# Softmax denominators by one weight sum per block, with three additions done by accumulating DMA transfers

## The chip, the cores and the metric

The kernel runs on one core of one Trainium2 chip. The metric is the device time of one execution in microseconds. The core's engines are TensorE (PE in the profile; PEld is its weight load), VectorE (DVE), ScalarE (ACT), GpSimd (POOL) and SyncE (SP), which only issues DMA transfers here. Each engine takes its instructions in the order of the program and waits on semaphores for the others.

## The reference, cut to what matters

Four layers follow one another on x of shape (16, 384, 16, 16), all in float32. The change is in the first, an attention over tokens, with 2 batches of 2048 tokens, 12 heads of 32 channels:

```python
xt = x.reshape(B, NUM_FRAMES, C, H, W).transpose(0, 2, 1, 3, 4)
xt = xt.reshape(B, C, N).transpose(0, 2, 1)
qk = (xt @ qk_w.T).reshape(B, N, 2, nh, HEAD_DIM)
...
attn = jax.nn.softmax(jnp.einsum('bhnd,bhmd->bhnm', q * scale, k), axis=-1)
attn = alpha * eye + beta * attn - gamma * Cm
out = jnp.einsum('bhnm,bhmd->bhnd', attn, v)
```

v is xt itself, and Cm is a matrix of 1/N, so the kernel computes alpha * x + beta * (exp(scores) v) / (sum of exp(scores)) - gamma * mean(x). The second layer (l1) is a depthwise 7x7 convolution, a LayerNorm and an MLP of 384 to 1536 to 384 with a response normalization; the third (l2) fuses gradients of the image through a 1x1 convolution; the fourth (l3a, l3b, l3c) holds 1x1 and 3x3 convolutions, a linear attention and a second MLP.

## The kernel before, in words

Channels lie on partitions, 3 groups of 128; tokens are the free dimension, in 4 blocks of 512 per batch. The kernel has two stages.

**Attention** (`attention`, from L398). A unit is a batch and a group of 4 heads; there are 6 units with 4 query blocks each, so 24 blocks. A block has 16 steps, one for each 128 keys. `scores` (L463) makes 4 matmuls, one per head, into two PSUM tiles of two banks (`pst`, three such tiles), and two exponentials on ACT, each over 1024 elements per partition. `weighted` (L481), run one step later so that ACT has time, multiplies by the values into `av`. In float32 each matmul is two MATMUL records in the profile, so a step has 8 records named st and 8 named av. For the softmax's denominator, DVE adds the exponentials of ADDS[n] successive steps, and `weights` (L524) lets PE multiply that sum by a matrix of ones into `dn`; ADDS gives 16, 8, 4 or 2 steps for each block, and a sum that is not the block's last one is multiplied in four quarters of 128 columns, spread over later steps. The sums use a pool of their own (`sp`, 4 tiles), the exponentials eight tiles of half a step (`ep`).

`finish` (L536) copies `dn` to SBUF on ACT, inverts it on DVE in four parts of 128 columns, scales the accumulated values and adds alpha * x. The dictionary `due` keeps work that is to be issued at a later step. `project` (L569) makes the queries and keys of blocks to come, two at a time, at step SLOT = 5 of a block, 12 MATMUL records; values come by DMA on SP's queue.

DVE would idle in part of this stage. So `fill` (L1481) puts work of the second layer there, after each step: one convolution task, and two `leads`, the l1 tasks of the first two images, whose LayerNorm starts at step LEAD. `pace` (L194) tells `fill` what a step costs PE and DVE by its own table, and what is left is filled.

**The rest.** Tasks of all 8 images are put into one order by a planner: each operation has an engine, a length and buffers that it takes and gives, and among the operations that can start soonest (within SLACK) the task of lowest RANK goes first. TURNS groups images that use the same MLP weights; `wa` and `wb` hold three chunks of 768 KB each, loaded by SP when their buffers come free. Within an engine the order of issue is then fixed; `InOrder` pins it, and its line (L96) is the line of nearly all records.

At the start, `first_loads` (L646) loads the first group's weights and then x, block by block, on SP's queue, and the vectors of scales and biases on ACT's.

```python
for n in range(NBLK):
    for t in range(NQC):
        es = scores(n, t)
        added = 0.0
        if before:
            before()
        before = lambda f=weighted, a=(n, t, es): f(*a)
        if t == SLOT and steps:
            added = project(f"p_{u}_{n}", steps[:2])
            del steps[:2]
        fill((u * NBLK + n) * NQC + t, added)
```

Of the kernel before, what the change touches and what calls it, by code (L numbers as in the profile page):

```python
# [9 lines left out]
F32 = mybir.dt.float32  # L10
# [3 lines left out]
PSUM = bass.MemoryType.PSUM  # L14

P = 128
# [15 lines left out]
SLOT = 5  # L32
LEAD = 20 * NQC + 6
# [12 lines left out]
RANK = {  # L46
    "mid": ((36.6, 22.0, 24.3, 85.6), (18.6, 42.9, 96.6, 26.9)),
    "l1": ((50.1, 89.5, 75.2, 4.0), (51.1, 16.8, 81.7, 28.5)),
    "l3c": ((45.7, 99.2, 100.9, 121.0), (-20.9, -6.3, 70.9, 62.0)),
    "conv": 109.4,  # L50
}
SLACK = 0.196
JUNK = 2

ADDS = (16, 8, 16, 16, 4, 4, 4, 2, 2, 8, 16, 16, 4, 16, 2, 4, 16, 8, 4, 4, 4, 4, 4, 4)
# [61 lines left out]
class Plan:  # L117
# [24 lines left out]
    def run(self, op):  # L142
# [9 lines left out]
        for tag, n in op.gives:  # L152
            self.room[tag] = sorted(self.room[tag] + [op.ready] * n)
# [40 lines left out]
def pace(t):  # L194


    n, i = divmod(t - 1, NQC)
    adds = ADDS[n]
    pe, dve = 2.066, 2.275 if t and i % adds else 0.0
    at = i - adds - 1  # L200
    parts = sum(j * adds // 4 == at % adds for j in range(4)) if at >= 0 else 0
    if parts:
        pe += 0.22 * parts
    elif i == 1 and n > 0:
        pe += 0.87
    else:
        pe += 0.09
    if n > 0:
        dve += {2: 0.88, 3: 0.88, 4: 0.88, 5: 0.88, 6: 0.6, 7: 0.66}.get(i, 0.0)
    return pe, dve  # L210
# [187 lines left out]
def attention(tc, X, xt, L0, block, small, col, cols, ones, load_qk, banks, fill, bound):  # L398
# [6 lines left out]
    with ExitStack() as actx:  # L405
# [48 lines left out]
        due = {}  # L454

        def unit(u, made, gm):
# [3 lines left out]
            adds = ADDS[u * NBLK : (u + 1) * NBLK]  # L460
            acc, sums = {}, {}

            def scores(n, t):  # L463
                es = []
                for i in range(2):
                    es.append(ep.tile([P, 2, BLK], F32, tag="e", name=f"e_{u}_{n}_{t}_{i}"))
# [10 lines left out]
                for i in range(2):  # L477
                    act.activation(es[i], sts[i], AF.Exp, scale=HD**-0.5)
# [1173 lines left out]
```

## Time and profile before

| | us |
|---|---|
| median of 3 runs | 2679.8 (2679.11 to 2679.9) |
| the profiled execution's own time | 2679.38 |
| its span | 2677.6 |
| PE busy | 2644.6 (99%) |
| DVE busy | 2011.5 (75%) |
| ACT busy | 1557.5 (58%) |
| POOL busy | 7.4 (0%) |
| exponentials e<-st, 768 of 128x1024 | 743.2 |
| additions s<-s,e and s<-e,e, 606 of 128x1024 | 513.3 + 191.0 |
| denominator matmuls dn<-s,ones | 2016 records |

The profile is one execution. Its groups name an operation as out<-in with its shape, the number of instructions, the busy time, the mean of one in ns, and then the idle time ahead of them with what ended it. Busy PE time is not all work: records of pipelined matmuls overlap, so the time of a step is read from the starts in the timeline.

### The profile page before, as it was taken

How to read it: one execution, taken by the hardware profiler on the slowest of the kernel's cores; microseconds unless marked ns; L12 is line 12 of the kernel's file. 1: busy time of each engine (PE TensorE's matmuls, PEld its weight loads, DVE VectorE, ACT ScalarE, POOL GpSimd, SP SyncE). 2: the span in 40 equal slices, each digit the busy share in tenths (PEclk: the TensorE clock that was granted, in tenths of full speed). 3: DMA queues.
4: the chain of work that ended last, by engine and by line, in shares of the span. 5: the costliest groups of instructions: out<-in, count | busy, mean ns of one | idle time of the engine just before them, and what ended most of it. 6: DMA issues, size and time to landing. Idle time of an engine off the chain costs nothing. (4 is left out here: it accounts for less than half of the span.)

```text
span 2677.6 us, 32803 instructions
## 1 busy us (share of the span) xinstructions
PE 2644.6 (99%) x12997; PEld 1061.5 (40%) x12997; DVE 2011.5 (75%) x2588; ACT 1557.5 (58%) x2314; POOL 7.4 (0%) x54
## 2 busy tenths in 40 slices
PE   8999999999999999899999999999999999999999
PEld 2223333233323323345444454444444444454443
DVE  5999999999999889999999999999652202732300
ACT  6787878878787888564565335457443542625201
POOL 0000000000000000000000000000000000000000
PEclk9999999999999999999999999999999999999999
DMA  3000000000000003000001001011001110000000
GB/s 150 5 13 1 9 9 5 13 1 5 13 1 1 1 13 108 23 0 0 1 1 47 25 12 31 29 36 36 24 24 36 47 36 24 0 1 1 12 17 20
DMA packets 28851, 55.69 MB, mean 21 GB/s; under 512 B 1680, under 2 KB 14096, under 8 KB 28688
## 3 DMA queue, kind: packets, MB, share of 16 engines
q1 hardware_dynamic: 28544, 53.35, 6.0%
q8 instruction: 104, 1.70, 0.3%
q14 instruction: 59, 0.48, 0.1%
q10 hardware_dynamic: 144, 0.15, 0.0%
HBM read 47.21 MB, written 6.29 MB: 20 GB/s over the span
## 5 line engine op out<-in xcount | busy, mean ns | idle before, releaser
L96 ACT ACTIVATE e<-st 128x1024 f32<-128x1024 f32 x768 | 743.2, 1025 | 88.5 <-PE st L96 80.7
L96 DVE SCALAR_TENSOR_TENSOR y<-l,vec,y 128x420 f32<-128x420 f32 (+8 forms) x1152 | 660.0, 638 | 5.0
L96 DVE TENSOR_TENSOR s<-s,e 128x1024 f32<-128x1024 f32 x444 | 513.3, 1216 | 11.7 <-ACT e L96 11.2
L96 PE MATMUL st<-q,k 32*128 32x512 f32 x3072 | 474.1, 641 | 4.0 <-ACT e L96 2.3
L96 PE MATMUL av<-e,v 128*32 128x512 f32 x3072 | 410.9, 606 | 4.3 <-ACT va L96 4.2
L96 PE MATMUL ph_l<-y,wa 128*128 128x512 f32 x576 | 261.4, 597 | 0.0
L96 PE MATMUL ph_l3c<-d_l3c,wa 128*128 128x512 f32 x576 | 258.4, 593 | 0.0
L96 PE MATMUL po_l<-hid_l,wb 128*128 128x512 f32 x576 | 255.7, 596 | 1.1 <-ACT hid_l L96 1.1
L96 PE MATMUL po_l3c<-hid_l3c,wb 128*128 128x512 f32 x576 | 256.6, 593 | 0.0
L96 PEld LDWEIGHTS st<-q,k 32*128 32x128 f32 x3072 | 146.1, 183 | 220.1 <-issue 132.4
L96 DVE TENSOR_TENSOR s<-e,e 128x1024 f32<-128x1024 f32 x162 | 191.0, 1221 | 54.7 <-ACT e L96 36.0
L96 ACT ACTIVATE hid_l<-ph_l,vec 128x512 f32<-128x512 f32 x96 | 66.0, 687 | 202.9 <-PE ph_l L96 202.8
L96 ACT ACTIVATE hid_l3c<-ph_l3c,vec 128x512 f32<-128x512 f32 x96 | 65.6, 687 | 202.6 <-PE ph_l3c L96 202.5
L96 PEld LDWEIGHTS av<-e,v 128*32 128x32 f32 x3072 | 60.6, 108 | 298.1 <-issue 274.0
L96 DVE SCALAR_TENSOR_TENSOR o_l3c<-po_l3c,vec,l 128x512 f32<-128x512 f32 x24 | 17.5, 748 | 209.6 <-PE po_l3c L96 208.8
L96 PEld LDWEIGHTS po_l<-hid_l,wb 128*128 128x128 f32 x576 | 109.5, 191 | 139.1 <-issue 128.0
L96 PEld LDWEIGHTS ph_l3c<-d_l3c,wa 128*128 128x128 f32 x576 | 108.8, 190 | 137.2 <-issue 133.4
L96 PEld LDWEIGHTS ph_l<-y,wa 128*128 128x128 f32 x576 | 109.1, 191 | 136.0 <-issue 125.1
L96 PEld LDWEIGHTS po_l3c<-hid_l3c,wb 128*128 128x128 f32 x576 | 109.0, 190 | 134.6 <-issue 132.8
L96 PE MATMUL p<-x,wqk_sb 128*128 128x512 f32 x288 | 132.3, 610 | 1.2 <-DMA x<-in_x_dram 1.2
L96 DVE SCALAR_TENSOR_TENSOR g_l3a<-h_l3a,dw,g_l3a 128x450 f32<-128x450 f32 (+1 forms) x192 | 119.0, 702 | 4.2 <-ACT g_l3a L96 4.1
L96 PEld LDWEIGHTS dn<-s,ones 128*32 128x32 f32 x2016 | 64.1, 110 | 125.4 <-issue 107.0
(155 smaller groups left out, 2446.3 us busy)
## 6 DMA issues: line engine op xcount, KB each, us to landing
wa<-in_w_dram SPq DMA_DIRECT2D x9, 768.0 KB, 4.5
wb<-in_w_dram SPq DMA_DIRECT2D x9, 768.0 KB, 5.0
wa<-in_mlp_w_dram SPq DMA_DIRECT2D x9, 768.0 KB, 4.4
wb<-in_mlp_w_dram SPq DMA_DIRECT2D x9, 768.0 KB, 4.5
x<-in_x_dram SPq DMA_DIRECT2D x8, 768.0 KB, 10.6
v<-in_xt_dram SPq DMA_DIRECT2D x24, 256.0 KB, 2.7
out_dram<-o_l3c SPq DMA_DIRECT2D x24, 256.0 KB, 2.1
qkv<-in_qkv_wT_dram SPq DMA_DIRECT2D x3, 576.0 KB, 11.1
```

Source lines behind the costliest of these rows:

```text
L96: self.last = self.tc.keep_in_program_order(make(*args, **kw))
```

## The change

- **One weight sum per block.** All 16 steps of a block are added up before PE multiplies once by ones. An exponential tile now holds a whole step (four heads, 2048 elements per partition), and there are six of them. The sum is built in place in step 2's tile.
- **Three additions by transfers.** The tiles of steps 1, 6 and 10 are added to those of steps 0, 5 and 9 by an accumulating DMA on GpSimd's queue; DVE merges the results into the sum at steps 6 and 10 and after the block's end (MERGED).
- **Banks.** PSUM is one pool of eight single banks, for scores, av, dn, projections and the second layer's statistics. Each head has an exponential of its own, of 512 elements.
- **Reciprocals.** The sums of a block, equal over the 32 rows of a head, go to DRAM and come back as a tile of 16 columns; that is inverted, written out and read back spread over the rows. The last block is divided in full instead.
- **Projections** move from step 5 to step 0 of a block; up to block PAIRED (21) the last merge, the denominator and `finish` of the block before follow them there; later blocks have these at steps 0 to 3 of the next block. The leads' ScalarE work (`fill` called with None) is issued ahead of them, and the first lead starts at step 17 * 16 + 1.
- **Start.** Keys' weights and x by channel group are loaded first; the vectors come on SP's queue; the batch-norm constants are computed after the loads are issued.
- **The rest of the kernel** has other TURNS (8 groups instead of 6), other RANK, SLACK and AFTER. A weight chunk of `wb` is given back by the user that comes last in the order, counted by `spent`.

The diff, cut to its core:

```diff
-SLOT = 5
-LEAD = 20 * NQC + 6
+PAIRED = (NB * NC - 1) * NBLK + 1
+LEAD = (17 * NQC + 1, 20 * NQC + 6)
 FIRST = NQC + 10
 TURNS = (
     (0, ((0, 0), (0, 1), (0, 2), (0, 3),)),
-    (1, ((0, 0), (0, 1),)),
-    (0, ((1, 0), (1, 2),)),
-    (1, ((0, 2),)),
-    (0, ((1, 1), (1, 3),)),
-    (1, ((1, 0), (0, 3), (1, 2), (1, 1), (1, 3),)),
+    (1, ((0, 0),)),
+    (0, ((1, 0),)),
+    (1, ((0, 1),)),
+    (0, ((1, 2), (1, 3),)),
+    (1, ((1, 0),)),
+    (0, ((1, 1),)),
+    (1, ((0, 2), (1, 2), (1, 1), (0, 3), (1, 3),)),
 )
-AFTER = ('x4', 0, 2)
+AFTER = ('x4', 0, 1)
...
-ADDS = (16, 8, 16, 16, 4, 4, 4, 2, 2, 8, 16, 16, 4, 16, 2, 4, 16, 8, 4, 4, 4, 4, 4, 4)
+MERGED = {0: 6, 5: 10, 9: NQC}
...
-        ep = pool("ep", 8)
-        sp = pool("sp", 4)
+        ep = pool("ep", 6)
         op = pool("op", 2)
-        pst = pool("pst", 3, space=PSUM)
-        pacc = pool("pacc", 1, space=PSUM)
-        def bank2(name):
-            return pst.tile([P, 2, BLK], F32, tag="st", name=name)
-        banks.append(lambda name: bank2(name)[:, 0, :])
-        fill(-1)
+        pb = pool("pb", 8, space=PSUM, reuse_waits="tile")
+        dp = pool("dp", 2, space=DRAM)
+        def bank(name):
+            return pb.tile([P, BLK], F32, tag="bank", name=name)
+        banks.append(bank)
...
+        due, behind, late = {}, [], []
         def unit(u, made, gm):
...
-            adds = ADDS[u * NBLK : (u + 1) * NBLK]
-            acc, sums = {}, {}
+            acc = {}
             def scores(n, t):
-                es = []
-                for i in range(2):
-                    es.append(ep.tile([P, 2, BLK], F32, tag="e", name=f"e_{u}_{n}_{t}_{i}"))
-                sts = [bank2(f"st_{u}_{n}_{t}_{i}") for i in range(2)]
+                es = ep.tile([P, 4, BLK], F32, tag="e", name=f"e_{u}_{n}_{t}")
+                sts = [bank(f"st_{u}_{n}_{t}_{h}") for h in range(4)]
                 for h in range(4):
...
-                for i in range(2):
-                    act.activation(es[i], sts[i], AF.Exp, scale=HD**-0.5)
+                for h in range(4):
+                    act.activation(es[:, h, :], sts[h], AF.Exp, scale=HD**-0.5)
                 return es
             def weighted(n, t, es):
                 if t == 0:
-                    acc["av"] = pacc.tile([P, BLK], F32, tag="av", name=f"av_{u}_{n}")
+                    acc["av"] = bank(f"av_{u}_{n}")
                 for h in range(4):
...
-                at = t % adds[n]
-                for i in range(2):
-                    if at == 0:
-                        sums[i] = es[i]
-                    elif at == 1:
-                        s = sp.tile([P, 2, BLK], F32, tag="s", name=f"s_{u}_{n}_{t}_{i}")
-                        dve.tensor_tensor(s, sums[i], es[i], ALU.add)
-                        sums[i] = s
+                block = u * NBLK + n
+                k = block * NQC + t
+                end = t == NQC - 1
+                pairs = [p for p in MERGED if MERGED[p] < NQC or block < NB * NC * NBLK - 1]
+                if t in pairs:
+                    acc[t] = es
+                elif t - 1 in pairs:
+                    nc.gpsimd.dma_start(acc[t - 1], es, accum_op=ALU.add)
+                    def merge(other=acc[t - 1], sums=acc):
+                        dve.tensor_tensor(sums[2], sums[2], other, ALU.add)
+                    when = MERGED[t - 1]
+                    if when == NQC and block < PAIRED:
+                        late.append(merge)
                     else:
-                        dve.tensor_tensor(sums[i], sums[i], es[i], ALU.add)
-                k = (u * NBLK + n) * NQC + t
-                if at == adds[n] - 1:
-                    parts = 1 if t == NQC - 1 else 4
-                    for i in range(parts):
-                        due.setdefault(k + 2 + i * adds[n] // 4, []).append(
-                            lambda i=i, summed=dict(sums): weights(
-                                n, t, summed, ts(i, BLK // parts)
-                            )
-                        )
+                        due.setdefault(block * NQC + when, []).append(merge)
+                elif t == 2:
+                    acc[2] = es
+                else:
+                    dve.tensor_tensor(acc[2], acc[2], es, ALU.add)
+                if end:
+                    f = lambda summed=acc[2]: weights(n, summed)
+                    if block < PAIRED:
+                        late.append(f)
+                    else:
+                        due.setdefault(k + 3, []).append(f)
                 for f in due.pop(k, ()):
                     f()
-                if t == NQC - 1:
+                if end:
...
-                    due[k + 2].append(lambda: finish(n, va, xg))
-            def weights(n, t, summed, at):
-                if t == adds[n] - 1 and at.start == 0:
-                    acc["dn"] = pacc.tile([P, BLK], F32, tag="dn", name=f"dn_{u}_{n}")
+                    (late if block < PAIRED else due[k + 3]).append(lambda: finish(n, va, xg))
+                    behind.extend(late)
+                    late.clear()
+            def weights(n, summed):
+                acc["dn"] = bank(f"dn_{u}_{n}")
                 for h in range(4):
                     pe.matmul(
-                        acc["dn"][HD * h : HD * (h + 1), at],
+                        acc["dn"][HD * h : HD * (h + 1), :],
                         ones[:, :HD],
-                        summed[h // 2][:, h % 2, at],
-                        start=(t == adds[n] - 1 and at.start == 0),
-                        stop=(t == NQC - 1),
+                        summed[:, h, :],
+                        start=True,
+                        stop=True,
                     )
             def finish(n, va, xg):
...
                 if g == 0:
                     L0[b][n] = block(f"l0_{b}_{n}")
                 k = u * NBLK + n
-                r = op.tile([P, BLK], F32, tag="r", name=f"r_{u}_{n}")
-                act.activation(r, acc["dn"], AF.Identity, accum_out=bound[:, 0, k : k + 1])
-                def invert(i):
-                    dve.reciprocal(r[:, ts(i, P)], r[:, ts(i, P)])
+                sums = op.tile([P, BLK], F32, tag="sums", name=f"sums_{u}_{n}", bufs=1)
+                act.activation(sums, acc["dn"], AF.Identity, accum_out=bound[:, 0, k : k + 1])
+                if k == NB * NC * NBLK - 1:
+                    r = op.tile([P, BLK], F32, tag="r", name=f"r_{u}_{n}", bufs=1)
+                    dve.reciprocal(r, sums)
+                    act.activation(sums, r, AF.Identity, accum_out=bound[:, 1, k : k + 1])
+                    dve.tensor_tensor(va, va, r, ALU.mult)
+                    dve.scalar_tensor_tensor(
+                        L0[b][n][:, g, :], va, col("beta", g), xg, ALU.mult, ALU.add
+                    )
+                    return
+                away = dp.tile([4, BLK], F32, tag="away", name=f"away_{u}_{n}")
+                nc.sync.dma_start(away, sums[0:P:HD, :])
+                few = op.tile([P, BLK // HD], F32, tag="few", name=f"few_{u}_{n}")
+                nc.sync.dma_start(few, away.rearrange("h (j k) -> (h j) k", j=HD))
+                r = op.tile([P, BLK], F32, tag="r", name=f"r_{u}_{n}", bufs=1)
+                def invert():
+                    dve.reciprocal(few, few)
+                    back = dp.tile([P, BLK // HD], F32, tag="back", name=f"back_{u}_{n}")
+                    nc.sync.dma_start(back, few)
+                    for h in range(4):
+                        nc.sync.dma_start(
+                            r[ts(h, HD)],
+                            back[ts(h, HD)]
+                            .rearrange("j k -> (j k)")
+                            .unsqueeze(0)
+                            .to_broadcast([HD, BLK]),
+                        )
                 def scale():
                     dve.tensor_tensor(va, va, r, ALU.mult)
-                def check():
-                    junk = op.tile([P, BLK], F32, tag="junk", name=f"junk_{u}_{n}", bufs=1)
-                    act.activation(junk, r, AF.Identity, accum_out=bound[:, 1, k : k + 1])
                 def put():
                     dve.scalar_tensor_tensor(
                         L0[b][n][:, g, :], va, col("beta", g), xg, ALU.mult, ALU.add
                     )
-                todo = [*(lambda i=i: invert(i) for i in range(TB)), scale, put]
-                for i, f in [*enumerate(todo), (8, check)]:
-                    due.setdefault((k + 1) * NQC + 2 + i, []).append(f)
+                def check():
+                    junk = op.tile([P, BLK // HD], F32, tag="bit", name=f"bit_{u}_{n}", bufs=1)
+                    act.activation(junk, few, AF.Identity, accum_out=bound[:, 1, k : k + 1])
+                first = (k + 1) * NQC + (0 if k < PAIRED else 3)
+                for i, f in ((2, invert), (4, check), (6, scale), (7, put)):
+                    due.setdefault(first + i, []).append(f)
...
         def project(name, steps):
-            pp = bank2(name)
-            for copy in [f(pp[:, i, :]) for i, f in enumerate(steps)]:
+            for copy in [f(bank(f"{name}_{i}")) for i, f in enumerate(steps)]:
                 copy()
             return 2.7 * len(steps)
...
+            if i == 0:
+                fill(-1)
...
                     if before:
                         before()
                     before = lambda f=weighted, a=(n, t, es): f(*a)
-                    if t == SLOT and steps:
-                        added = project(f"p_{u}_{n}", steps[:2])
-                        del steps[:2]
+                    if t == 0 and steps:
+                        fill((u * NBLK + n) * NQC, None)
+                        many = 1 if len(steps) == NBLK - 1 else 2
+                        added = project(f"p_{u}_{n}", steps[:many])
+                        del steps[:many]
+                    for f in behind:
+                        f()
+                    behind.clear()
                     fill((u * NBLK + n) * NQC + t, added)
...
     def first_loads(t):
-        load_qk(t, [0])
-        for n in range(NBLK):
+        nc.sync.dma_start(t[:, 0, 1], wqk[0][:, 1])
+        for c in range(NC):
+            nc.sync.dma_start(X[0][0][:, c, :], x[0, 0][:, c, :])
+        nc.sync.dma_start(t[:, 0, 0], wqk[0][:, 0])
+        nc.sync.dma_start(vec, vecs)
+        for n in range(1, NBLK):
             load_x(0, n)
...
-    nc.scalar.dma_start(vec, vecs)
+        norms()
...
+    bn = [tuple(const.tile([P, NC], F32, name=f"{t}_{k}") for t in ("sc", "sh")) for k in (1, 2)]
...
+    def norms():
+        for (sc, sh), k, bias in zip(bn, ("L3_bn1_", "L3_bn2_"), (None, "L3_db")):
+            nc.scalar.activation(sc, cols(k + "v"), AF.Sqrt, bias=eps5)
...
+    def spent(first, k):
+        uses[first, k] = uses.get((first, k), 0) + 1
+        return int(uses[first, k] == len(TURNS[first][1]))
...
-                gives=[("s", 1)] + ([("wb", 1)] if last and f % NG == NG - 1 else []),
+                gives=[("s", 1)] + ([("wb", lambda: spent(first, k))] if f % NG == NG - 1 else []),
...
+            if added is None:
+                room = 2.5
+                for task in leads:
+                    while task.head.engine == "ACT" and task.rest <= t and room >= task.head.length:
+                        room -= 2.5 if task.head.table else task.head.length
+                        if not plan.step(task):
+                            break
+                        task.rest = t if task.head.engine == "ACT" else t + 1
+                return
...
-            for task in (*leads, conv):
-                if task.rest > t or t < (FIRST if task is conv else LEAD):
+            for task, since in zip((*leads, conv), (*LEAD, FIRST)):
+                if task.rest > t or t < since:
                     continue
                 before = None
                 while task is not conv or ("y", 0, YB - 1, NC - 1) not in plan.made:
                     op = task.head
+                    if op.engine == "ACT" and task is not conv:
+                        break
                     if before and before.engine != op.engine:
                         task.rest = t + 1 + (before.engine == "DVE")
                         break
                     if op.engine == "DVE":
-                        if free < max(0.4, op.length - 1.5):
+                        bank = any(tag == "mm" for tag, _ in op.gives)
+                        if free < max(0.4, op.length - 1.5) and not bank:
                             break
                         free -= op.length + 0.12 * (before in op.after)
                     if not plan.holds(task, "wa") or not plan.step(task):
```

More of the change, by code (lines that the diff above doesn't have):

```diff
@@ L985, in hidden, with second @@
         return hid, made
[L987 removed]
+    uses = {}
+    def spent(first, k):
+        uses[first, k] = uses.get((first, k), 0) + 1
+        return int(uses[first, k] == len(TURNS[first][1]))
+    def second(hid, first, name, ready, before=None):
         po = []
@@ L1432, in layer3c @@
         )
-        po, m = yield from second(hid, at, n, made, last)
+        po, m = yield from second(hid, at, n, made)
         for c in range(NC):
```

74 lines of the change are left out of this document (32 added, 42 removed).

## The prediction, made before the changed kernel ran

> **What bounds the kernel now.** I read busy time first: TensorE works through the whole span, so only TensorE time that goes counts.
>
> ```profile
> PE 2644.6 (99%) x12997; PEld 1061.5 (40%) x12997; DVE 2011.5 (75%) x2588; ACT 1557.5 (58%) x2314; POOL 7.4 (0%) x54
> ```
>
> Then the busy time in three stretches: before the first score matmul (22.07), attention up to its last denominator matmul (1052.34), and the rest.
>
> ```profile
> 0.00:22.07 22.07, 16.14 (x32) 7.06 (x32) 3.27 (x19) 3.92 (x7) 0.70 (x6) 1.00 0.93 369
> 22.07:1052.34 1030.27, 1021.94 (x8423) 318.45 (x8423) 962.66 (x1013) 837.38 (x992) 0.00 (x0) 1.00 0.03 8
> 1052.34:2677.60 1625.26, 1606.48 (x4545) 735.98 (x4543) 1045.59 (x1556) 716.17 (x1315) 6.74 (x48) 0.99 0.08 24
> ```
>
> The columns are length, PE, PEld, DVE, ACT, POOL, clock, DMA share, GB/s. In attention PE, DVE (93%) and ACT (81%) are all close to full, and the DMA engines are idle (0.03). The change works here. Next, the groups by shape, for the denominator and for what stands beside it:
>
> ```profile
> L96 ACT ACTIVATE e<-st 128x1024 f32<-128x1024 f32 x768 | 743.2, 1025 | 88.5 <-PE st L96 80.7
> L96 DVE TENSOR_TENSOR s<-s,e 128x1024 f32<-128x1024 f32 x444 | 513.3, 1216 | 11.7 <-ACT e L96 11.2
> ...
> L96 PE MATMUL dn<-s,ones 128*32 128x128 f32 x1824 | 84.3, 273 | 0.0
> ...
> L96 PE MATMUL dn<-s,ones 128*32 128x512 f32 x192 | 26.7, 612 | 0.0
> ```
>
> Matmul records overlap, so busy times do not price a step. Start times do. Two stretches of the PE timeline, one in a block that sums once (ADDS 16), one in a block that sums four times (ADDS 4):
>
> ```profile
> 148.61 1.31 PE L96 MATMUL st<-q,k 32*128 32x512 f32 x8
> 150.20 1.07 PE L96 MATMUL av<-e,v 128*32 128x512 f32 x8 [0.28 <-ACT va L96]
> 151.19 1.74 PE L96 MATMUL st<-q,k 32*128 32x512 f32 x8
> 152.86 1.07 PE L96 MATMUL av<-e,v 128*32 128x512 f32 x8
> 153.75 1.04 PE L96 MATMUL dn<-s,ones 128*32 128x512 f32 x8
> 154.72 1.14 PE L96 MATMUL st<-q,k 32*128 32x512 f32 x8
> ...
> 161.09 5.42 PE L96 MATMUL p<-x,wqk_sb 128*128 128x512 f32 x12
> 166.44 1.14 PE L96 MATMUL st<-q,k 32*128 32x512 f32 x8
> ...
> 168.50 1.31 PE L96 MATMUL st<-q,k 32*128 32x512 f32 x8
> ...
> 170.74 1.14 PE L96 MATMUL st<-q,k 32*128 32x512 f32 x8
> ```
> ```profile
> 989.40 1.14 PE L96 MATMUL st<-q,k 32*128 32x512 f32 x8
> 990.48 1.06 PE L96 MATMUL av<-e,v 128*32 128x512 f32 x8
> 991.36 0.40 PE L96 MATMUL dn<-s,ones 128*32 128x128 f32 x8
> 991.69 1.14 PE L96 MATMUL st<-q,k 32*128 32x512 f32 x8
> ```
>
> A step of scores and weighted values costs 2.06 (166.44 to 168.50). The next one costs 2.24: its score matmuls wait 0.17 for a bank that ACT still reads. With a quarter of a denominator it costs 2.29 (989.40 to 991.69), 0.22 over a clean step of 2.07. At the start of a block, ACT's copy of av and its xg hold the two steps from 148.61 for 0.5 and 0.6.
>
> **The sum, against the profiled execution:** 2679.4 us, a span of 2677.6 and 1.8 around it; the median of the three runs, 2679.8, lies 0.4 above.
>
> *Weight sums.* ADDS makes 81 sums in 24 blocks; 24 stay, 57 go, each in 4 quarters of 8 matmuls (57 x 32 = 1824, the row). 228 x 0.22 = **-50**. They lie on the path, since PE is the bound. The 24 last ones (153.75 to 154.72, 0.97 each) stay.
>
> *Banks.* Three double tiles become eight single ones; av and dn draw from them, so seven serve the scores. Only the fourth score matmul of a step then needs a bank of the step before, 2 us old. The other 384 - 228 = 156 steps lose half of 0.17: **-13**. ACT must keep up: four copies of 512 follow each other at about 0.48 (two copies of k took 1.07, one takes 0.59), 1.93 a step against 2.07. It does, with 0.14 to spare instead of 0.23.
>
> *Projections at step 0.* PE then works 5.35 (161.09 to 166.44) just where ACT copies av and makes xg, and av's next bank is another one. The 1.1 at the start of a block goes in the 22 blocks that have projections: **-24**. In the same way ACT's normalization: at 968 to 982 it loaded the square-root table and the exponential's again (1.28 each), and three steps, a quarter and a whole denominator took 14.5 instead of 7.4, PE at half pace after it: **-7**.
>
> *What is added on PE's path.* The denominator of a block waits for the last addition and one merge. The last exponentials end about when step 0 begins; addition and merge take 2 x 2.28 (0.69, 1.22, 1.76 for 512, 1024, 1536, so 2.28 for 2048), with some 1 of arrears 5.7; PE comes there after av and projections, 1.0 + 5.35 after its scores, 1.0. Hidden by 1.6; if that cover goes, each us late costs 24 in all, because every score matmul stands behind it. In the last block nothing covers it: **+2**.
>
> *DVE.* 606 additions of 1024 (704 us) become 289 of 2048 (659); four reciprocals of 128 (88.7 in all) become 23 tiny ones. The order of the changed kernel shows the room filled again: 290 convolution steps before the end of attention instead of 256. DVE: 659 + 290 x 0.62 (159.4 over 259 there now) + 24 x 1.44 (scaling and output) + 15 (means, the rest) = 888 of about 960, as full as before.
>
> *Transfers.* 71 transfers of 1 MiB on the POOL queue, empty until now; nothing stands behind them there. The source tile is written again 5, 4 and 4 steps later, by ACT's exponentials, and behind those stand all later exponentials, and PE. From the last exponential of the source to that write are 4 x 2.07 + 0.3 - 2.2 = 6.4; PE's weighted values give 0.9 more. So PE loses what the landing takes over **7.3** (9.4 for the first transfer). No row shows an accumulating transfer. The nearest:
>
> ```profile
> wa<-in_w_dram SPq DMA_DIRECT2D x9, 768.0 KB, 4.5
> ...
> x<-in_x_dram SPq DMA_DIRECT2D x8, 768.0 KB, 10.6
> ```
>
> At 369 GB/s (first stretch) 768 KB move in 2.1, so 2.4 is fixed. 1 MiB moved once: 2.8 + 2.4 = 5.2. Read twice, as an addition must: 8.1. Queued behind others: 10.6. The price per block is 0 at 5.2, 1.6 at 8.1 (two transfers late by 0.8), 7.8 at 10.6. I take 1.0, between the first two and nearer to the second: 24 x 1.0 = **+24**.
>
> The Trainium skill (DMA: Bandwidth & Descriptors, "Anatomy of one DMA - SWDGE (gpsimd) path") gives 2.0 us and bytes over 436e3 for such a queue: an estimate of 4.4, or 6.8 with two reads, as Collectives: The Full Stack ("The bandwidth ceiling") finds that a reduction is held by its two source reads; the sum would be 24 lower. Against the change speaks SBUF - State Buffer ("SBUF: two separate sides"): a GpSimd queue's descriptors are held up while VectorE runs an instruction that uses both its port pairs. By that page additions of two tensors are no such instructions, and those fill DVE here; no row shows either.
>
> *SP's queue.* Per block a sum goes out, comes back, and after the reciprocal goes out and is spread: about 2.1 a transfer (the out row's landing). v's loads stand among them on SP and are needed a unit later: nothing.
>
> *Start.* The first projection needs 192 + 256 KB instead of 384 + 768; at 369 GB/s that is 1.9 earlier. The small vectors now land later; only the bias preparation behind the first two projections waits for them: **-2**.
>
> *After attention.* The matmuls are the same. Between 1084 and 1097 PE waited 3.65 + 1.93 + 2.13 for a second block's normalization, which the changed order has ready sooner: **-6**. Two more weight groups (12 loads of 4.5) and new ranks are worth between -10 and +15; I take 0, since PE waited for no weights in this stretch.
>
> Sum: -50 - 13 - 24 - 7 + 2 + 24 - 2 - 6 = -76: 2679.4 - 76 = **2603**.
>
> **Rivals.**
> *DVE sets the pace.* Its waits grow: 70 merges, 23 reciprocals and 23 scalings each wait for a DMA. Busy 888, plus the 67.6 it idled before, plus 116 x 0.4 = 1002 for attention instead of 1030 - 70 = 960: **2645**. For it: 93% busy already. Against it: PE waited for DVE almost never before, and merges come 4 to 6 steps after their transfers start.
> *Transfers land late (slower).* At 10.6, the x row, ACT waits at steps 6, 10 and 14: 2 x 3.3 + 1.2 = 7.8 a block, 187 in all, in place of the 24: **2766**. It decides from the point at which the gain of 100 without transfer losses is eaten: 4.2 a block, 2.1 for each of the two short ones, a landing at **9.4**. For it: reads double and 1 MiB is more than any transfer here. Against it: the DMA engines are otherwise idle.
> *Nothing comes of it:* a landing near 9.4, or ACT (1536 exponentials, 1.93 of 2.07) loses the 70 again: **2679**. That the sums don't go can't be: the changed order has 24 denominators.
>
> **How the numbers follow.** Forecast 2603 (2580 to 2625): 0.60. DVE's pace (2625 to 2660): 0.22. Slower by transfers (2690 to 2770): 0.12. Within 0.2% (5.4 us, about what a measurement of this kernel can tell from no change): 0.03. The remaining 0.03 is faster, between 2660 and 2674. Faster 0.85, same 0.03, slower 0.12. The range 2575 to 2660 holds the first two; the low end is the forecast without transfer losses.
>
> **What would show it.** Right: attention some 70 shorter; no quarter denominators; score matmuls at 2.07 without the alternating 0.17; projections right after the first scores of a block, with ACT's av and xg copies beside them; exponentials of steps 6, 10 and 14 waiting for a DMA by less than 1 us; no table load ahead of an idle PE. Wrong: transfers that land later than 8.1; denominators waiting for DVE in every block; ACT the releaser of score matmuls in most steps; weight loads releasing PE after attention.

## The result, and the profile after

The changed kernel took **2696.3 us** (median of 4 runs, 2691.6 to 2701.3), the kernel before 2679.5 beside it: a ratio of 1.0070, 95% interval 1.0056 to 1.0084. It is 0.7% slower; the forecast was 2603, with a range up to 2660. The profiled execution took 2691.64, a span of 2689.8. Times below are medians; one of five runs of the kernel called pairs took 3773.25 at a granted clock of 0.653, in a slow state of the chip, and is left out.

Busy time on the page of the changed kernel, and then the same three stretches as before (up to the first score matmul, attention up to the first matmul after its last denominator, the rest), with the columns named in the prediction:

```profile
PE 2644.5 (98%) x11173; PEld 1017.9 (38%) x11173; DVE 1908.8 (71%) x2199; ACT 1612.7 (60%) x3097; POOL 68.6 (3%) x125
```
```profile
0.00:18.86 18.86, 14.84 (x32) 6.38 (x32) 3.47 (x19) 3.99 (x7) 0.69 (x6) 1.00 0.90 343
18.86:1059.30 1040.44, 1023.78 (x6601) 274.86 (x6600) 882.72 (x663) 876.05 (x1760) 61.23 (x71) 0.99 0.41 87
1059.30:2689.80 1630.50, 1605.88 (x4545) 736.70 (x4541) 1022.65 (x1517) 732.62 (x1330) 6.73 (x48) 1.00 0.09 30
```

PE has 1824 records fewer and is as long "busy" as before: busy records that overlap and wait inside a group hide what happened, so the windows must be read for length. The start is 3.2 shorter, attention 10.2 longer (1030.27 to 1040.44), the rest 5.2 longer. The forecast had attention at about 962; that is where it failed.

The costliest two groups of the page and, from its list of transfers, the new one (KB each, median us from issue to landing):

```profile
L100 ACT ACTIVATE e<-st 128x512 f32<-128x512 f32 x1536 | 787.9, 618 | 99.0 <-DMA e<-e 51.3
L100 DVE TENSOR_TENSOR e<-e,e 128x2048 f32<-128x2048 f32 x289 | 662.0, 2291 | 113.9 <-ACT e L100 56.0
...
e<-e POOLq DMA_DIRECT2D x71, 1024.0 KB, 7.1
```

The DVE row is what the prediction computed (289 at 2.28; it had 659). The ACT row is new in its last column: the exponentials waited 51.3 us for the transfers. In the timeline of ACT and of the POOL queue, block 3 of the changed kernel:

```profile
165.86 8.39 ACT L100 ACTIVATE e<-st 128x512 f32<-128x512 f32 x16
175.56 4.03 ACT L100 ACTIVATE e<-st 128x512 f32<-128x512 f32 x8 [1.31 <-PE av L100]
...
184.96 4.03 ACT L100 ACTIVATE e<-st 128x512 f32<-128x512 f32 x8 [0.96 <-DMA e<-e]
```
```profile
168.22 0.86 POOL L498 DMA_DIRECT2D e<-e  x1 [9.82 <-PE st L100]
```

Step 6's four exponentials end at 167.93; POOL starts the transfer 0.29 later; it lands at 175.46, 7.24 after its issue; and at 175.56 ACT goes on, into the tile that the transfer has just read. ACT had been ready at 174.25, 6.3 after step 6. (The releaser named is PE's av, but the weighted values of this tile had run from 167.85 to 169.03; the landing stands 0.1 ahead of the start.) PE in the same place:

```profile
173.21 1.14 PE L100 MATMUL st<-q,k 32*128 32x512 f32 x8
...
175.28 2.05 PE L100 MATMUL st<-q,k 32*128 32x512 f32 x8
...
178.65 1.14 PE L100 MATMUL st<-q,k 32*128 32x512 f32 x8
```

From 175.28 to the next scores at 178.65 are 3.37 instead of 2.07: PE loses 1.30, all of ACT's 1.31. The same happens behind the transfer of step 10.

The second loss is smaller and everywhere. Steps of block 3 that no transfer touches:

```profile
156.09 1.14 PE L100 MATMUL st<-q,k 32*128 32x512 f32 x8
157.16 1.18 PE L100 MATMUL av<-e,v 128*32 128x512 f32 x8
158.28 1.14 PE L100 MATMUL st<-q,k 32*128 32x512 f32 x8
159.35 1.07 PE L100 MATMUL av<-e,v 128*32 128x512 f32 x8
160.34 1.14 PE L100 MATMUL st<-q,k 32*128 32x512 f32 x8
```

The steps still alternate, 2.19 (156.09 to 158.28) and 2.06. The bank wait of the score matmuls is gone, as predicted, but now the weighted values wait: a group takes 1.18 instead of 1.07, since its fourth head needs the fourth exponential. The four heads' scores run side by side and end together; the first exponential starts 1.16 after their start (median of all steps), the next ones follow at 0.477, and the fourth lasts 0.62. The fourth exponential so ends about 3.2 after the scores' start at best (3.22 in most steps of this block). PE comes to it at 2.07 + 1.07 = 3.14. As a rate ACT keeps up: in the row at 175.56, where it is late, eight exponentials, two steps' worth, follow each other in 4.03, less than two steps of 2.07. It is the way through the loop, from scores to weighted values, that is too long by some 0.1.

### The profile page after: what moved, and what is told of

It reads as the page before. It is cut to its first block, busy times and chain, and to the rows that moved or that the text cites. A ratio compares the mean times of both kernels' runs of the same rounds, so it can differ in the third digit from the quotient of the medians.

```text
span 2689.8 us, 29424 instructions
## 1 busy us (share of the span) xinstructions
PE 2644.5 (98%) x11173; PEld 1017.9 (38%) x11173; DVE 1908.8 (71%) x2199; ACT 1612.7 (60%) x3097; POOL 68.6 (3%) x125
## 4 chain that ended last, share of the span: by engine, by line
PE 53%; DVE 5%; ACT 2%; DMA 0%; issue 0%; DVEq 0%; ACTq 0%
PE ph_l3c L100 9%; PE ph_l L100 8%; PE po_l L100 8%; PE po_l3c L100 8%; PE pf_l L100 4%; DVE y L100 2%; PE pp_l3b L100 2%; PE pq_l3b L100 2%; PE pd_l3a L100 2%; PE pk_l3b L100 2%; PE pv_l3b L100 2%; PE pc_l3a L100 2%; DVE g_l3a L100 1%; PE pn_l3b L100 1%; PE pkv_l3b L100 1%; DVE s_l L100 1%
## 5 line engine op out<-in xcount | busy, mean ns | idle before, releaser
L100 ACT ACTIVATE e<-st 128x512 f32<-128x512 f32 x1536 | 787.9, 618 | 99.0 <-DMA e<-e 51.3
L100 DVE TENSOR_TENSOR e<-e,e 128x2048 f32<-128x2048 f32 x289 | 662.0, 2291 | 113.9 <-ACT e L100 56.0
L100 PE MATMUL st<-q,k 32*128 32x512 f32 x3072 | 479.9, 642 | 9.9 <-ACT e L100 9.6
L100 PE MATMUL av<-e,v 128*32 128x512 f32 x3072 | 454.3, 606 | 0.0
L100 PEld LDWEIGHTS st<-q,k 32*128 32x128 f32 x3072 | 137.0, 183 | 356.7 <-issue 288.6
L100 PEld LDWEIGHTS av<-e,v 128*32 128x32 f32 x3072 | 85.8, 108 | 311.1 <-issue 273.5
L100 ACT ACTIVATE kp_l3b<-pk_l3b,minus 128x384 f32<-128x384 f32 x32 | 18.6, 580 | 145.8 <-PE pk_l3b L100 145.7
```

The source lines that it names most:

```text
L100: self.last = self.tc.keep_in_program_order(make(*args, **kw))
```

## The experiments

All steps below are means over blocks 1 to 19, in us from one start of scores to the next. Step 0 includes the projections and the denominator; "others" are steps 1 to 10 and 12 to 14.

| kernel | time | ratio to before, 95% interval | a block | step 0 | step 11 | step 15 | others |
|---|---|---|---|---|---|---|---|
| changed | 2696.3 | 1.0070 (1.0056 to 1.0084) | 43.46 | 8.42 | 3.46 | 3.22 | 2.18 |
| pairs | 2697.4 | 1.0059 (1.0042 to 1.0076) | 43.87 | 8.48 | 3.42 | 3.08 | 2.22 |
| **seven** | **2645.9** | **0.9879 (0.9863 to 0.9896)** | 41.48 | 8.82 | 2.12 | 2.17 | 2.18 |
| pairs_seven | 2653.1 | 0.9902 (0.9886 to 0.9919) | 41.89 | 8.75 | 2.11 | 2.12 | 2.22 |
| six_lean | 2695.5 | 1.0065 (1.0049 to 1.0082) | 43.45 | 8.46 | 3.42 | 3.36 | 2.17 |
| half | 2636.6 | 0.9838 (0.9821 to 0.9854) | 41.05 | 8.51 | 2.22 | 2.19 | 2.16 |
| dve_all | 2850.1 | 1.0642 (1.0624 to 1.0659) | 41.44 | 9.29 | 2.10 | 2.13 | 2.15 |
| seven_lag | 2716.7 | 1.0135 (1.0117 to 1.0152) | 45.37 | 7.53 | 2.45 | 2.08 | 2.56 |
| eight_lag | 2737.9 | 1.0229 (1.0211 to 1.0248) | 45.00 | 7.46 | 2.07 | 2.07 | 2.57 |
| seven_dn1 | 2645.3 | 0.9881 (0.9864 to 0.9897) | 41.57 | 7.65 | 2.14 | 2.12 | 2.28 |
| eight_in | 2671.9 | 0.9976 (0.9965 to 0.9987) | 41.73 | 7.42 | 2.07 | 3.14 | 2.24 |
| seven_pool | 2661.4 | 0.9943 (0.9926 to 0.9960) | 42.30 | 8.77 | 2.12 | 2.17 | 2.25 |
| oldplan | 2810.1 | 1.0485 (1.0468 to 1.0503) | 43.70 | 8.52 | 3.56 | 3.36 | 2.17 |

Two theories stood at first. **Transfers:** they come back too late for six tiles. **ScalarE:** four exponentials of 512 fill a step and leave no slack. The first three kernels set them against each other.

### pairs: exponentials of 1024 again

```diff
-sts = [bank(f"st_{u}_{n}_{t}_{h}") for h in range(4)]
-for h in range(4):
-    act.activation(es[:, h, :], sts[h], AF.Exp, scale=HD**-0.5)
+sts = [bank2(f"st_{u}_{n}_{t}_{i}") for i in range(2)]      # three double tiles, as before
+for i in range(2):
+    act.activation(es[:, 2 * i : 2 * i + 2, :], sts[i], AF.Exp, scale=HD**-0.5)
```

> The changed kernel with the exponentials back in pairs of heads: two of 1024 elements a step instead of four of 512, PSUM divided as before (three double tiles, one bank each for av and dn). Everything else is as changed. Theory ACT: four exponentials take 0.52 each, 2.09 a step, no slack against PE's 2.07, so every delay of ACT stays and the transfers' waits become PE's; with two of 0.92 (1.84 a step) ACT catches up, a landing of 7.1 stays within 7.3, and a block falls from 43.5 to about 40.3: 2616 us (2600 to 2635). Theory transfers: the tiles of steps 6, 10 and 14 come free too late whatever ACT does, so the 2.4 us a block that steps 11 and 15 lose remain and only the 1.5 of the other steps goes: 2656 us (2645 to 2670).

Nothing was gained: 2697.4, and both expectations (2616 and 2656) missed. The timeline of ACT in block 3 shows why:

```profile
179.01 3.77 ACT L100 ACTIVATE e<-st 128x1024 f32<-128x1024 f32 x4 [1.62 <-DMA e<-e]
```

With cheaper exponentials ACT is ready earlier, and waits longer for the same landing. Steps 11 and 15 stay long, and the other steps get the bank wait back (2.22). ScalarE's pace is not what makes steps 11 and 15 long.

### seven, pairs_seven and six_lean: one more tile

```diff
-ep = pool("ep", 6)
+ep = pool("ep", 7)
-xg = op.tile([P, BLK], F32, tag="xg", name=f"xg_{u}_{n}")
+xg = L0[b][n][:, g, :]                      # written where its result goes
-va = op.tile(..., tag="va", ...)
+va = op.tile(..., tag="va", ..., bufs=1)    # and one scratch tile shared
```

> The changed kernel with seven exponential tiles instead of six; the room comes from alpha * x being written straight into the output block and from single buffers for two small tiles. A source of a transfer is then written again a step later. Theory transfers: the 2.4 a block go, 2634 us (2620 to 2645). Theory ACT: the waits for DMA go too, but ACT stays the pace with 36.8 us of work a block and 3.9 of waiting for projections: 41 a block, 2632 us at best, and more likely about 2650, as its arrears then show elsewhere. The two agree on the direction; what tells is whether the steps other than 11 and 15 stay at 2.17 (ACT) or fall to 2.07 (transfers).

> Both edits. Theory ACT: no better than the pairs alone, 2616 us. Theory transfers: 2.4 and 1.5 a block go, 2595 to 2605 us, some 50 below the pairs alone.

The windows of the kernel with seven tiles, attention and the rest:

```profile
19.38:1012.00 992.62, 979.04 (x6597) 263.56 (x6600) 881.92 (x663) 879.22 (x1760) 61.38 (x71) 1.00 0.44 94
1012.00:2643.60 1631.60, 1606.25 (x4549) 736.58 (x4541) 1022.83 (x1517) 733.81 (x1330) 6.78 (x48) 1.00 0.09 29
```

Attention is 47.8 shorter than in the changed kernel, the rest the same. Steps 11 and 15 are ordinary. From step 6 of block 3 to step 0 of block 4, all exponentials stand in one row, without a wait that the profile lists:

```profile
161.06 23.43 ACT L100 ACTIVATE e<-st 128x512 f32<-128x512 f32 x44
```

Exponentials wait 3.5 us for transfers between 60 and 900 us, where it was 41.2. The landing is 7.1 as before: the transfers are not faster, they have a step more. **This version beats both kernels**, by 1.2% against the one before. The time lies between the two expectations: the waits for transfers went, as the theory of transfers had it, but the other steps stayed at 2.18, as the theory of ScalarE had it, so the second loss is untouched. With the pairs on top it is 0.3% slower again, and both expectations for that kernel (2616, and 2595 to 2605) missed.

The edits that make room for the tile could have done it themselves, so they were run with six:

> Control for the seven tiles: the same edits that make room for the seventh (normalized input written into its L0 block, one va tile, shared scratch), but six tiles. Theory: it is the tile that counts, the waits for transfers at steps 11 and 15 stay, and the time is that of the changed kernel, 2696 within 8. Rival: the edits themselves gave the 50 (one copy fewer in flight, other waits): 2660 or less with six tiles as well.

2695.5: it is the tile.

### half: a shorter transfer, six tiles

```diff
-nc.gpsimd.dma_start(acc[t - 1], es, accum_op=ALU.add)
+nc.gpsimd.dma_start(acc[t - 1][:, :2, :], es[:, :2, :], accum_op=ALU.add)
```

> The changed kernel with six tiles, its transfers add two of the four heads only (512 KB instead of 1 MiB; the additions of the other two heads are left out). Theory of the late landing: a landing of 7.1 falls to about 4.7 (half of the part over the fixed 2.4), the source is free in time, the waits of exponentials for a DMA and the long steps 11 and 15 go, the rest stays: 2696 - 48 = 2648, as with seven tiles. Rival, the tile is held by something other than the bytes (the issue, or a fixed delay): steps 11 and 15 stay over 2.8, 2680 or more.

```profile
e<-e POOLq DMA_DIRECT2D x71, 512.0 KB, 4.5
```

This kernel leaves out the additions of two heads, so its 2636.6 is no time for the whole work. The list of transfers has 4.5 for half the bytes, and the long steps are gone with six tiles too. So it is the landing against the time to the next write, from either side. 7.1 and 4.5 make 2.6 per 512 KB and 1.9 fixed. The Trainium skill (DMA: Bandwidth & Descriptors, "Anatomy of one DMA - SWDGE (gpsimd) path") states a fixed part of 2.0, which agrees; with the source and the destination both read at its 436 KB per us, an estimate from that page, 512 KB more would take 2.4 (measured 2.6). The estimate of 6.8 in the prediction was the good one, and 4.4, with the bytes counted once, was not.

### dve_all: no transfers at all

```diff
-MERGED = {0: 6, 5: 10, 9: NQC}
+MERGED = {}        # all 15 additions of a block on DVE, and its pace told so
```

> The changed kernel with six tiles and no transfers: all 15 additions of a block on VectorE (360 of 2.28 instead of 289), one denominator a block. Theory that the transfers are what costs: the stalls at steps 11 and 15 (about 2 a block) go, and VectorE's 15 x 2.28 + 1.4 = 35.6 a block fits into 40.5 to 41.5; convolution work that then finds no room (about 71 x 2.28 = 162 of VectorE) moves behind attention, where VectorE is 64% busy: 2650 to 2670. Rival, VectorE's time is what the transfers had to save: the moved work lengthens the time after attention by a good part of 162, or the denominators wait for VectorE in each block: 2720 or more.

Attention and the rest, and the longest wait of PE after attention:

```profile
19.33:1010.60 991.27, 967.38 (x6595) 257.76 (x6594) 878.97 (x472) 871.04 (x1746) 0.00 (x0) 1.00 0.05 16
1010.60:2847.60 1837.00, 1626.28 (x4547) 744.72 (x4547) 1186.16 (x1779) 711.77 (x1318) 6.86 (x48) 0.94 0.08 27
```
```profile
PE su_l L100 <- DVE s_l L100: 117.9, 2, 117.2
```

The first theory was right for attention (991, steps 11 and 15 ordinary), the rival for the whole. With 71 more additions on VectorE, 36 instructions of the convolutions (y) are left in attention where the changed kernel has 295; the others now stand between attention and the first tasks that need them, and PE stands idle for 117 us at once. The granted clock is 0.50 from 1004.9 to 1172.1, around that wait. So the transfers earn their place: each takes an addition of 2.29 off VectorE, and an addition took 2291 ns with transfers beside it and without. What they held up was the tile that they read, and small transfers beside them (last section).

### seven_lag, eight_lag, eight_in: room in the chain

```diff
-if before:
-    before()
-before = lambda f=weighted, a=(n, t, es): f(*a)
+if len(before) == 2:          # weighted values two steps behind the scores
+    before.pop(0)()
+before.append(lambda f=weighted, a=(n, t, es): f(*a))
```

> Seven exponential tiles, and the weighted values of a step come one step later on TensorE (after the scores of the step after next instead of the next). Theory of the chain: with seven tiles a step takes 2.17 on average, not 2.07, since the scores of four heads end together 1.12 after their start, the four exponentials take 3 x 0.48 + 0.62 = 2.06, and TensorE comes to the weighted values 2.07 + 1.07 = 3.13 after the start of the scores: 1.12 + 2.06 = 3.18, so there is no room, and whatever else ScalarE does is paid by TensorE. One step later there are 2.07 of room: the 13 steps outside 0, 11 and 15 go from 2.17 to about 2.08, 1.2 a block, 28 in all. But a tile then lives a step longer, so the transfers hold up the steps near 11 and 15 again, about 2 a block, 48: 2646 - 28 + 48 = 2666. Rival, ScalarE's own pace: its exponentials and copies fill the steps whatever the order; the steps stay at 2.17 and the stalls come back: 2694.

> Eight exponential tiles and the weighted values one step later; the room for the eighth tile comes from four of the 22 small tiles of the convolutions (18 left), which can move the time after attention by some 10 either way. Theory of the chain: no stalls at steps 11 and 15, as with seven tiles, and the other steps at 2.08 instead of 2.17: 2646 - 28 = 2618, the attention part about 28 shorter than with seven tiles. Rival, ScalarE's own pace: steps stay at 2.17, 2646.

The PE timeline of eight_lag in block 1:

```profile
70.87 1.14 PE L100 MATMUL st<-q,k 32*128 32x512 f32 x8
71.94 1.06 PE L100 MATMUL av<-e,v 128*32 128x512 f32 x8
72.94 1.14 PE L100 MATMUL st<-q,k 32*128 32x512 f32 x8
74.01 1.07 PE L100 MATMUL av<-e,v 128*32 128x512 f32 x8
```

Scores start every 2.07 and the groups of weighted values take 1.06 or 1.07, with no wait in them: the alternation is gone, and steps 9, 11 and 13 are 2.07 in the mean, the others from step 5 on 2.07 to 2.20. Of steps 3 to 15 in blocks 1 to 19, 89% are at 2.07, against 26% in seven. That is what the chain says and what its rival denied. The sums of both kernels were wrong all the same (2666 and 2618 expected, 2716.7 and 2737.9 measured): steps 0 to 2 of a block in eight_lag became 7.46 + 6.44 + 3.62, where seven has 8.82 + 2.07 + 2.24, 4.4 more. With the lag, PE stands at the denominator waiting for VectorE: 53.1 us in 17 waits between 60 and 900 us, against 7.0 in 7 in seven. After most of these waits the granted clock is 0.50 for 3.4 to 10.2 us, and the matmuls there are longer: from 111.7 to 115.1, for one, where the denominator took 1.52 instead of 1.07 (block 1) and the scores after it 2.09 instead of 1.14. In seven_lag the tile's longer life brings the waits for transfers back besides (step 10: 3.06, step 13: 3.41).

eight_in keeps the lag inside a block and gives up the lag at its ends; the denominator fills step 1, which has no weighted values.

> Eight tiles (18 small ones instead of 22), weighted values one step later, but only inside a block: at step 0 TensorE has caught up and keeps its cover, and the denominator fills the gap of step 1, which has no weighted values. Theory of the chain: steps 2 to 14 at 2.07 as with eight tiles and the lag throughout, and without its 4.4 us at the start of a block: about 39.4 to 40 a block instead of 45.0, attention ending near 1013 - 24 x 1.7 = 972 (against 1013 with seven tiles); the rest 29 longer, as with 18 small tiles before: 2602 + 29 = 2631. Rival, the start of a block is held by ScalarE whatever stands there: 43 a block or more, 2690 or slower.

The block fell to 41.73, between the two expectations and not under seven's 41.48: steps 3 to 14 gain 0.7 together, steps 0 to 2 are 13.13 together (7.42 + 2.80 + 2.91), as in seven, and step 15, which carries two groups of weighted values, is 3.14. The rest is 26 longer (1658 against 1632), here and in eight_lag, the two kernels that give up four small tiles.

### seven_dn1, seven_pool: the start of a block

> Seven tiles, and the denominator of a block comes one step later on TensorE, after the scores of step 1 and ahead of the weighted values of step 0; what follows it (sum, reciprocal, scaling) moves by a step too. Theory: with seven tiles step 0 takes 8.82 instead of 8.06 since the denominator waits for VectorE's last addition and merge (21.8 in 17 waits); a step later they have 2.07 more, steps 0 and 1 together fall from 10.89 to about 10.15: 22 x 0.75 = 16, 2646 - 16 = 2630. Rival, ScalarE's load at the start of a block (four copies of av, k or q, and the sum) is what holds steps 0 and 1 to 4, and moving the denominator only moves the wait to step 1 or 2: 2646 within 4.

Step 0 fell by 1.17, and steps 1 and 3 grew by 1.00 and 0.49. The wait only moved, and the time stayed at 2645.3, as the rival had it.

```diff
-act.activation(xg, X[b][n][:, g, :], AF.Identity, scale=col("alpha", g), bias=gm)
+nc.gpsimd.tensor_scalar(xg, X[b][n][:, g, :], col("alpha", g), gm, ALU.mult, ALU.add)
```

> Seven tiles, and the normalized input of a block (xg, 128x512) is made on GpSimd instead of ScalarE. Theory that ScalarE's load at the start of a block is what holds steps 0 to 4 (10.92 of them over 9 us for steps 0 and 1, a denominator placed later gained nothing): one of its five 0.5 us copies there goes, the blocks get about 0.4 shorter, 41.5 to 41.1, 2646 - 24 x 0.4 = 2636. Rival, the hold comes from the chain of scores, exponentials and weighted values alone, which has no room whatever stands around it: 2646 within 4. Against both: GpSimd's instruction could slow VectorE beside it (additions over 2.29) or hold up the transfers issued behind it on its queue: over 2650.

Steps 0 to 11 are those of seven within 0.05: this one copy less on ScalarE at the start of a block is worth nothing measurable. The other four copies stayed, so ScalarE's load there is not ruled out; what holds the first steps in full stays open. One part can be read in seven: in 6 of blocks 1 to 19 the denominator waits for VectorE, 0.24 in the mean of the 0.43 by which step 0 exceeds 8.39. The 13.7 us between the two spans (2643.6 and 2657.3) were lost in one piece, on POOL's timeline:

```profile
494.66 17.36 POOL L527 TENSOR_SCALAR l<-x,vec,gm 128x512 f32<-128x512 f32 x12 [8.68 <-issue]
511.97 1.61 POOL L499 DMA_DIRECT2D e<-e  x2
```

POOL had no order written out; the twelve copies of the second batch were all put where their bias came ready, two transfers stood behind them, and an exponential waited 14.3 us for the first. An addition of VectorE beside them (at 502.67) took 2.70 instead of 2.29. How far a better placed copy would gain was not tried.

### oldplan: the tables of the rest

> The changed kernel with the weight groups, ranks and slack of before (TURNS, AFTER, RANK, SLACK). After attention the changed kernel took 1630.5 us, before took 1625.3. Theory plan: the new ranks cost some 5 to 10 us here, so 2682 to 2687. Theory attention: the stretch is longer since work arrives otherwise and PE starts it cold after a wait for the last sum; the old ranks give 2692 or more.

Attention has the same steps; the rest became 119 longer than in the changed kernel (1749.4 against 1630.5); the waits of PE there are many, the longest in total 13.0 for one kind of activation, 11.7 and 10.5 for two kinds of results of VectorE. The time is over the 2692 of the second theory, but for a reason that neither named: the old order of the rest does not fit what the changed attention leaves undone, so this run does not say which of the new ranks cost 5 us.

## Why the prediction was wrong, step by step

The forecast lay 88.6 below the profiled execution (2691.6). Where that comes from:

| step of the prediction | it had | measured | missing, us |
|---|---|---|---|
| transfers | +24 | attention 1040.4 against 992.6 with a seventh tile: 47.8 | 24 |
| banks: steps at 2.07 | clean | seven's steps 1 to 15: 2.177, 15 x 0.107 x 24 | 39 |
| step 0 | 2.07 + 5.35 + 0.97 = 8.39 | seven's 8.82: 22 x 0.43 | 9 |
| end of attention | 5.8 + 2 | 11.7 (last scores 1047.57, next matmul 1059.31) | 4 |
| the rest | -6 | +5.2 | 11 |
| start | -2 | -3.2 | -1 |

Together these are 86 of the 88.6.

**Transfers: the limit was wrong, not the landing.** The prediction bounded the landing at 5.2 to 8.1, and 7.1 lies inside. By its own limit of 7.3 that would have cost nothing; the 24 it took was a middle between two cases, not a price of this one. The limit had two parts. The 6.4 from the last exponential to the next write was right (6.3). The 0.9 that "PE's weighted values give" did not exist: PE lost as much as ACT, 1.30 of 1.31. And 0.29 from the exponential to POOL and 0.1 from the landing to ACT were left out. The limit is about 6.3 - 0.4 = **5.9**; a landing of 7.2 is 1.3 late, twice a block. The first transfer, with five steps, was in time, as predicted: landed at 164.55, its tile written at 165.86.

**Banks: the wait was replaced, not removed.** The prediction had that "four copies of 512 follow each other at about 0.48", 1.93 a step, with 0.14 to spare. The rate was right: eight took 4.03 where ACT was late, and a late step's first exponential follows the one before at 0.48 like the others. What failed is to take the rate for the test. PE needs a step's fourth exponential 3.14 after the start of its scores, and that one ends at 3.22, however much ACT has to spare. Before, the score matmuls waited 0.17 in every second step; after, the weighted values wait 0.12. The sum's -50 and -13 both counted on steps of 2.07; 39 of these 63 are missing. In seven the eight records of a group of weighted values start over 0.56 in the mean, 0.47 where nothing holds them: that is 0.085 of the 0.107. eight_lag shows the step at 2.07 once they need not wait. The same tight link is why there was no 0.9 of slack behind a late exponential.

**Step 0.** In the changed kernel it was as predicted: 8.42 against 8.39. The 9 in the table appear only when the transfers are in time, as in seven, where PE comes to some denominators before VectorE is done (0.24 of the 0.43).

**What held.** The quarters are gone: 1824 records fewer. With the transfers in time a block falls from 43.01 to 41.48, and to 41.05 with half transfers. VectorE was busy 882.7 in attention (888 computed), and between 60 and 900 us a denominator of the changed kernel waited for it once, 1.2: DVE's rival fell. Normalization: the block with the second one (block 22) fell from 44.27 to 39.98, with late transfers in it, and to 35.94 in seven. The rival of late transfers had the right mechanism and place, exponentials that wait at steps 10 and 14. It let this decide only from a landing of 9.4, worked out from the limit of 7.3, and its own case, a landing of 10.6, did not come. That the time lies in its range of 2690 to 2770 is partly luck: of the 86 above, the transfers make 24.

**The end of attention.** In the last block nothing lies between the weighted values and the denominator:

```profile
1048.64 3.25 PE L100 MATMUL av<-e,v 128*32 128x512 f32 x16
1057.45 1.94 PE L100 MATMUL dn<-e,ones 128*32 128x512 f32 x8 [5.56 <-DVE e L100]
```

PE idles 5.56 until VectorE has ended six additions in a row (1043.12 to 1057.39), where 2 were allowed. From 1055.1 to 1061.9 the granted clock is 0.50, and the matmuls there run slower (four in 3.26).

**The rest: open.** PE is busy as long as before (1605.88 and 1606.48 in the windows), so the 5.2 are waits. The largest kind is for a hidden activation, 8.5 in three waits against 1.1 in two before; the longest, 3.67 at 1193.44, stands on ScalarE behind 2.21 us of another task's scaling. The waits that the prediction wanted gone (7.7 between 1084 and 1097) shrank; the largest near them are 0.9 and 2.5 (at 1099.28 and 1102.20), and others came with the new order. Which table entry makes them was not settled.

## What to carry to other kernels

A buffer that a transfer reads is free one landing after its issue, plus what lies around it: compare that with the time until the *same buffer* is written again, and grant no slack to the engines behind unless a row shows it. If an added transfer comes late by less than a step, one more buffer removes the wait as a shorter transfer does, and can be paid by writing a small result where it must go anyway. Before a wait is counted as removed, lay out the whole loop (matmul, exponential, next matmul) and add up the time through it, not only each engine's rate: 3.22 against 3.14 was enough to bring the wait back.

## What the runs showed of the hardware

- An accumulating transfer within SBUF took 7.1 for 1 MiB (median of 71, from 6.9 to 9.2) and 4.5 for 512 KB, from issue to landing, and 0.86 of POOL's time to issue; VectorE's additions beside it took 2291 ns, the same as without it.
- Exponentials of 128x512 from PSUM started every 0.477 where they had nothing to wait for, within a step and from one step to the next, though each lasts about 0.6; 1024 elements in one instruction took 1.03 in the kernel before.
- Small transfers were held up beside the large ones: in block 3 of the changed kernel 8 KB written at 158.85 were read only from 164.73 on. The median landing of these 8 KB was 6.3 beside transfers of 1 MiB, 2.5 beside 512 KB and 1.4 in dve_all, without any.
- After waits of PE the granted clock stood at 0.50 for 3.4 to 10.2 us in most blocks of eight_lag (waits of 1.1 to 4.0), and for 6.8 us at the end of attention in the changed kernel (5.56 of wait), but not after the 3.67 at 1193.44.
